# Strassen's seven products in the first MLP matmul of a fused vision block

## The chip, the cores and the metric

The kernel runs on one core of a Trainium2 chip. The core has a matmul engine (TensorE, PE in the profile), two elementwise engines that can read the matmul's result memory PSUM (VectorE, DVE; ScalarE, ACT), one that works on SBUF only in this kernel (GpSimd, POOL), and a queue that issues most DMAs (SyncE, SP). Each engine works through its own instructions in program order, and waits on semaphores for what others produce. The metric is the device time of one execution in microseconds (us); lower is better.

## The reference

Two transformer-like layers work on an image batch of 2 x 56 x 56 tokens with 384 channels, all in float32. The first is neighbourhood attention and an MLP. The second is a convolution with four running averages, a projection, and an MLP. Its end, which is where the change lies, is this:

```python
mixed = 0.25 * (lr + rl + tb + bt) + local            # 768 channels per token
mixed = _layernorm(mixed, on_g, on_b)
x = x + (mixed @ w_out + b_out)                       # 768 -> 384
h2 = _layernorm(x, n2_g, n2_b)
m = jax.nn.gelu(h2 @ w1 + b1, approximate=False) @ w2 + b2   # 384 -> 1536 -> 384
return x + m
```

## The kernel before

The 6272 tokens of the second layer's end are cut into groups (`dgroups`): twelve of 512 tokens, which are four token tiles of 128, and a last one of 128. The loop over groups is at lines 1614 to 1645 for groups 0 to 5 and at lines 1659 to 1684 for groups 6 to 12 (`half_way` is 6). For each group g there are four pieces of work:

- **The hidden layer.** `hT` holds the normalized input of the group with channels on the partitions, three blocks of 128 channels. `columns` (L1092) makes one tile of 128 hidden channels by 512 tokens in a PSUM bank: three matmuls, one per channel block, with a 128x128 piece of `w1` as weights and 512 columns of `hT`. `hidden` then has ScalarE apply the gelu (L1103). There are twelve such tiles. From group 6 on they are made in an order (L1664) that completes two tiles of the lower half of the hidden channels and two of the upper half together, because `sums_of_hidden` (L1526) has GpSimd make sums of these for the second matmul.
- **Measuring.** Beside the hidden layer of group g, the mean and variance of `mixed` are taken for the tokens of group g + 1. From group 7's tokens on this is `measure_by_vector` (L1315): VectorE turns each token tile in sixteen 32-row transposes (L1320) and takes two statistics (L214) and one aggregate (L215). `Norm.close` turns variances into factors: one VectorE instruction (L219), then a power on GpSimd (L222).
- **`project_out`** (L1341) multiplies `mixed` of group g + 1 by `w_out`, token tile by token tile (L1110), adds the residual on VectorE with the measured factor (L1347), and measures the result for the next norm.
- **`tokens_by_seven`** (L1533) is the second matmul of the MLP of group g. It already uses Strassen's seven block products, with the blocks being halves of the tokens, of the hidden channels and of the output channels. Between these products it prepares the next group's `hT`: ScalarE normalizes (L240), VectorE transposes (`turned`, L1076), ScalarE scales by the norm's gain and bias (`scaled`, L1083). It ends with adds into the result and one output DMA.

The program order within each engine is written out by hand: the order of the Python calls is the order of the instructions. A PSUM bank that is named again waits for its last reader. Before group 6 the PSUM pools are rearranged (L1647 to 1658): one bank, `bank_b`, is written to zero by a matmul with zeros, so that later matmuls may add to what ScalarE copies into it. The GpSimd sums of `w2` for the seven products are made at the start of group 5 (`sums_of_w2`, L1516), behind the add of a row to the next input tile (`add_row`, L1028).

Of the kernel before, what the change touches and what calls it, by code (L numbers as in the profile page):

```python
# [33 lines left out]
F32 = mybir.dt.float32  # L34
AF = mybir.ActivationFunctionType
# [7 lines left out]
P = 128  # L43
# [130 lines left out]
def block_kernel(ctx: ExitStack, tc: tile.TileContext, ins: dict, out: bass.AP):  # L174
# [26 lines left out]
    class Norm:  # L201
# [12 lines left out]
                nc.vector.bn_stats(st[:n, i, :], x)  # L214
            nc.vector.bn_aggr(self.mv[:n, k, :], st[:n, : len(parts), :])  # L215

        def close(self, k, n=P):
            rs = self.rs[:n, :k]
            nc.vector.scalar_tensor_tensor(  # L219
                rs, self.mv[:n, :k, 1], EPS, ones[:n, :k], ALU.add, ALU.mult  # L220
            )
            nc.gpsimd.tensor_tensor(rs, rs, mhalf[:n, :k], ALU.pow)  # L222

        def apply(self, k, x, out):
            n = x.shape[0]
# [755 lines left out]
    def passes(xs, xn, w1, w2, between=lambda ps: None):  # L981
# [32 lines left out]
        def bank():  # L1014

            turns.append(0)
            in_turn = bank_b is None and len(turns) % 2 == 1
            return y_end if in_turn else ps_y.tile([P, C], F32, name="y")

        turns, hids, bank_b = [], [], None  # L1020

        def row(name):
            return rows[:, 1 if name == "b_out" else 0, :]
# [61 lines left out]
                    scale=col(g, c),  # L1085
                )

        def columns(w, m, hT, n):

            ps = ps_m.tile([P, MT], F32, name="mm")  # L1090
            for c in range(NC):
                nc.tensor.matmul(  # L1092
                    ps[:, : n * P], lhsT=w[:, c, m * P : (m + 1) * P], rhs=hT[:, c, : n * P],
                    start=c == 0, stop=c == NC - 1,
                )
            return ps

        def hidden(w1, m, hT, n, b1):
            ps = columns(w1, m, hT, n)
# [214 lines left out]

        def measure_by_vector(mx, norm, k):  # L1315

            t = tp.tile([P, NI * P], F32, name="turned", bufs=2)
            for i in range(0, P, HD):
                for j in range(0, P, HD):
                    nc.vector.transpose(  # L1320
                        t[j : j + HD].rearrange("p (m c) -> p m c", m=NI)[:, :, i : i + HD],
                        mx[i : i + HD, :, k * P + j : k * P + j + HD],
                    )
            norm.add(k, [t[:, h * C : (h + 1) * C] for h in range(2)])

        def measure_beside(m, g, ahead):


            n = dgroups[g][1]
            if g > half_way:  # L1330
                if m % 2 == 0 and m // 2 < n:
                    measure_by_vector(ahead[0], ahead[2], m // 2)
            else:
                late = 2 if g == half_way else 0
                k = (m - late) // 2 - 1
                if m % 2 == 1 and 0 <= k < n:
                    measure(ahead[0], ahead[2], k)
            if m == (NHID - 1 if g == half_way else 10):
                ahead[2].close(n)

        def project_out(g, mx, x, inner):  # L1341
            n = dgroups[g][1]
            x3 = io.tile([P, NT, C], F32, name="xc")
            norm = Norm(sm)
            for k in range(n):
                ps = tokens([mx[:, c, :] for c in range(NI)], w_out, k)
                nc.vector.scalar_tensor_tensor(  # L1347
                    x3[:, k, :], ps, inner.rs[:, k : k + 1], x[:, k, :], ALU.mult, ALU.add
                )
                norm.add(k, [x3[:, k, :]])  # L1350
                beside.go(OUT_D)
            norm.close(n)
            return x3, norm
# [159 lines left out]
        project_in(g, hT, first_input)  # L1513
        n2 = "L1_conv_n2_g", "L1_conv_n2_b"

        def sums_of_w2(w2):  # L1516

            q = NHID // 2
            b11, b12 = w2[:, :q, : C // 2], w2[:, :q, C // 2 :]
            b21, b22 = w2[:, q:, : C // 2], w2[:, q:, C // 2 :]  # L1520
            t1, t2, t3, t4 = (tp.tile([P, q, C // 2], F32, name=f"w2_t{i}") for i in range(4))
            for to, x, y in ((t1, b12, b11), (t2, b22, t1), (t3, b22, b12), (t4, b21, t2)):
                nc.gpsimd.tensor_tensor(to, x, y, ALU.subtract)
            return t1, t2, t3, t4
# [8 lines left out]
        def tokens_by_seven(t0, low, high, s1, s2, w2, w2_sums, res, g, x_next, norm):  # L1533
# [8 lines left out]
            bank_a = ps_d.tile([P, 2, hc], F32, name="ya")  # L1542
# [3 lines left out]
            more = g + 1 < dlast  # L1546
# [53 lines left out]
            for p in range(2):  # L1600
                product(bank_b, p, of(high, 1), t4)
            scaled(hT, n_next, *n2)
            add_row(x_next, n_next, "b2_1")
            nc.vector.tensor_tensor(quarter(1, 0), bank_b, quarter(1, 0), ALU.add)
            for p in range(2):
# [6 lines left out]
            return hT  # L1612
        hT = channels(first["xn"], dgroups[0][1], *n2)
        for g, (t0, n) in enumerate(dgroups[:half_way]):
            if g == half_way - 1:

                cctx.close()
                tp = pctx.enter_context(tc.tile_pool(name="tail", bufs=1, reuse_waits="tile"))
                w2_sums = sums_of_w2(w2)
            hid = []  # L1620
            for m in range(NHID):
                hid.append(hidden(w1, m, hT, n, "L1_conv_b1"))
                measure_beside(m, g + 1, ahead)
                beside.go(MLP_D)
            res = x3
            x3, norm = project_out(g + 1, *ahead)
            if g + 2 != half_way:
                ahead = load_mix(g + 2)
            for k in range(n):
                if k == n - 1:  # L1630
                    hT = channels(xn, dgroups[g + 1][1], *n2)
                ps = tokens(hid, w2, k)
                o = res[:, k, :]
                if k == 0:
                    norm.shift(dgroups[g + 1][1])
                nc.vector.tensor_tensor(o, ps, o, ALU.add)
# [8 lines left out]


        bctx.close()  # L1647
        ps_y = pctx.enter_context(tc.tile_pool(name="psy2", bufs=2, space=PSUM))
        ps_m = pctx.enter_context(tc.tile_pool(name="psm2", bufs=3, space=PSUM))
        ps_d = pctx.enter_context(tc.tile_pool(name="psd", bufs=1, space=PSUM))  # L1650
        HALVES, HC = 2, C // 2
        bank_b = ps_d.tile([P, HALVES, HC], F32, name="yb")
        zeros = tp.tile([P, C], mybir.dt.bfloat16, name="zeros")
        nc.vector.memset(zeros, 0.0)

        nc.tensor.matmul(
            bank_b.rearrange("p t c -> p (t c)"), lhsT=zeros[:, :P], rhs=zeros, start=True, stop=True
        )
        for g, (t0, n) in enumerate(dgroups):
            if g < half_way:  # L1660
                continue
            hid = {}
            first_pair = len(hids)
            for i, m in enumerate(m for u in range(3) for m in (2 * u, 2 * u + 1, 6 + 2 * u, 7 + 2 * u)):  # L1664
                hid[m] = hidden(w1, m, hT, n, "L1_conv_b1")
                if g < dlast:
                    measure_beside(i, g + 1, ahead)
                    if i % 4 == 3:
                        if i == 3:
                            s1, s2 = (tp.tile([P, NHID // 2, MT // 2], F32, name=x) for x in ("s1", "s2"))  # L1670
                        sums_of_hidden(i // 4, *hids[-2:], s1, s2)
            res = x3
            if g < dlast:
                x3, norm = project_out(g + 1, *ahead)
            if g + 2 <= dlast:
                ahead = load_mix(g + 2)
            if g == dlast:
                for k in range(n):
                    ps = tokens([hid[m] for m in range(NHID)], w2, k, y_end)
                nc.vector.tensor_copy(rows[:, 1, :], res[:, n - 1, :])  # L1680
                assert n == 1 and t0 + n * P == T2
                break
            pairs = hids[first_pair:]
            hT = tokens_by_seven(t0, pairs[::2], pairs[1::2], s1, s2, w2, w2_sums, res, g, x3, norm)
        pctx.close()

    def raise_flag(ps):
# [89 lines left out]
```

## Time and profile before

| | us |
|---|---|
| Median of 3 runs (2639.23 to 2642.07) | 2639.56 |
| The profiled execution, whole | 2640.17 |
| Its span in the profile | 2638.4 |

Busy time in single groups of the second half of the loop, from the stage view of the profile (from one group's first matmul to the next group's):

| group | stretch, us | PE | DVE | ACT | POOL | PE clock |
|---|---|---|---|---|---|---|
| 6 | 2188.41 to 2262.09 | 73.68 | 55.69 | 13.26 | 25.34 | 1.00 |
| 8 | 2335.78 to 2409.45 | 73.67 | 56.54 | 14.38 | 26.33 | 1.00 |
| 10 | 2483.13 to 2556.81 | 73.68 | 54.18 | 15.45 | 23.86 | 1.00 |
| 11 | 2556.81 to 2618.88 | 62.07 | 15.43 | 11.45 | 19.48 | 1.00 |

Columns are microseconds in which the engine was busy. Group 11 is shorter because the group after it has only one token tile to project. Busy time of PE is that of pipelined records: how fast matmuls follow each other is read from start to start. Rows of the profile name the source line, the engine, the operation, the tile written and the tiles read, the shapes, and how many instructions are merged; in square brackets stands the idle time of the engine before the row and what ended it.

### The profile page before, as it was taken

Reading aid. Unit: us, or ns where it says so; the run is one execution under the profiler, and the core shown is the slowest. Engines: PE = TensorE matmul, PEld = TensorE weight load, DVE = VectorE, ACT = ScalarE, POOL = GpSimd, SP = SyncE. Lnnn points to the kernel's source line nnn. Section 1 sums busy time; section 2 is a strip of 40 time slices with the busy share of each in tenths; the row PEclk is TensorE's granted clock in tenths of the full one; section 3 lists DMA queues with packets and bytes.
Section 4 is the critical chain, followed back from the end, with each engine's and each line's share of the span. In section 5 each row is a group of like instructions: output and inputs, shape, how many; then the busy total and the mean of one; then the engine's idle time right before and its main releaser. Section 6 shows DMA issues by size and latency. Waiting matters only on the chain. (4 is left out here: it accounts for less than half of the span.)

```text
span 2638.4 us, 38178 instructions
## 1 busy us (share of the span) xinstructions
PE 2613.8 (99%) x15420; PEld 1520.5 (58%) x15420; DVE 1961.9 (74%) x3540; ACT 906.9 (34%) x1465; POOL 365.6 (14%) x370
## 2 busy tenths in 40 slices
PE   9999999999999999999999999999999999999999
PEld 5666556666655445555555555555555555666777
DVE  3778777876465688688988889889988825788761
ACT  4555555554323333223334423212233311122111
POOL 0111111110211100000010000000010032333332
PEclk9999999999999999999999999999999999999999
DMA  6423354224511122233345535533264321111000
GB/s 217 138 91 98 125 185 162 81 81 144 180 37 39 64 90 102 95 116 111 121 142 214 209 125 184 181 119 120 102 220 164 143 94 42 48 48 48 22 12 17
DMA packets 131644, 299.05 MB, mean 113 GB/s; under 512 B 10390, under 2 KB 86528, under 8 KB 129152
## 3 DMA queue, kind: packets, MB, share of 16 engines
q1 hardware_dynamic: 126512, 269.76, 29.8%
q10 hardware_dynamic: 4944, 26.74, 2.9%
q8 instruction: 123, 2.02, 0.3%
q14 instruction: 65, 0.53, 0.1%
HBM read 180.86 MB, written 115.61 MB: 112 GB/s over the span
## 5 line engine op out<-in xcount | busy, mean ns | idle before, releaser
L1092 PE MATMUL mm<-hT,w 128*128 128x512 f32 (+3 forms) x1872 | 769.5, 568 | 0.4 <-ACT hT L254 0.2
L1092 PEld LDWEIGHTS mm<-hT,w 128*128 128x128 f32 x1872 | 346.4, 190 | 386.8 <-issue 364.7
L1103 ACT ACTIVATE hid<-mm,chan 128x512 f32<-128x512 f32 (+3 forms) x312 | 206.1, 661 | 659.5 <-PE mm L1092 659.5
L1188 DVE SCALAR_TENSOR_TENSOR loc<-pt,taps,loc 128x990 f32<-128x990 f32 (+9 forms) x336 | 377.1, 1122 | 10.0 <-ACT loc L1170 1.7
L1110 PE MATMUL y_end<-w,hid 128*128 128x384 f32 x912 | 300.3, 486 | 0.0
L1110 PE MATMUL y<-w,hid 128*128 128x384 f32 x864 | 284.5, 486 | 0.0
L222 POOL TENSOR_TENSOR rs<-rs,mhalf 128x4 f32<-128x4 f32 (+4 forms) x67 | 87.3, 1303 | 1418.7 <-DVE rs L219 1383.3
L531 DVE TENSOR_TENSOR pts<-sc,bias 119x448 f32<-119x448 f32 (+3 forms) x336 | 220.8, 699 | 72.1 <-PE sc L516 70.0
L537 ACT ACTIVATE pts<-pts 119x448 f32<-119x448 f32 (+3 forms) x336 | 206.6, 642 | 183.4 <-DVE pts L531 183.3
L1110 PEld LDWEIGHTS y_end<-w,hid 128*128 128x128 f32 x912 | 172.7, 190 | 118.8
L1110 PEld LDWEIGHTS y<-w,hid 128*128 128x128 f32 x864 | 163.5, 190 | 112.5 <-issue 1.0
L387 PE MATMUL ps<-hT,wqkv 128*128 128x448 f32 x504 | 211.9, 559 | 7.1 <-ACT vs L432 5.0
L1076 DVE STREAM_TRANSPOSE hT<-xn 32x96 f32<-32x96 f32 x672 | 181.2, 270 | 38.1 <-ACT xn L240 17.7
L1092 PE MATMUL mm<-hT,w_in 128*128 128x512 f32 (+2 forms) x468 | 191.9, 568 | 0.6 <-ACT hT L254 0.6
L1092 PEld LDWEIGHTS mm<-hT,w_in 128*128 128x128 f32 x468 | 88.5, 190 | 102.1 <-issue 90.4
L387 PEld LDWEIGHTS ps<-hT,wqkv 128*128 128x128 f32 x504 | 90.0, 190 | 87.8 <-issue 72.2
L1110 PE MATMUL y<-w_out,mx 128*128 128x384 f32 x420 | 138.7, 486 | 0.0
L516 PEld LDWEIGHTS sc<-qT,kT 32*100 32x100 f32 (+3 forms) x3168 | 90.7, 169 | 66.9 <-issue 15.5
L1320 DVE STREAM_TRANSPOSE turned<-mx 32x192 f32<-32x192 f32 x336 | 123.3, 367 | 4.2
L240 ACT ACTIVATE xn<-xc,sh,rs 128x384 f32<-128x384 f32 x98 | 64.7, 698 | 168.4 <-DVE sh L233 168.3
L516 PE MATMUL sc<-qT,kT 32*100 32x112 f32 (+3 forms) x3168 | 113.4, 270 | 6.5 <-DVE pts L531 5.2
L1110 PEld LDWEIGHTS y<-w_out,mx 128*128 128x128 f32 x420 | 79.7, 190 | 57.7 <-issue 5.3
(134 smaller groups left out, 3104.3 us busy)
## 6 DMA issues: line engine op xcount, KB each, us to landing
loc<-loc_d SPq DMA_DIRECT2D x24, 784.0 KB
mixed<-mix_d SPq DMA_DIRECT2D x24, 784.0 KB
mix_d<-mixed SPq DMA_DIRECT2D x24, 784.0 KB
xa<-x_d SPq DMA_DIRECT2D x23, 768.0 KB
bias<-in_bias_t ACTq DMA_DIRECT2D x13, 1344.0 KB
mx<-mix_d SPq DMA_DIRECT2D x11, 1536.0 KB
p_d<-mx SPq DMA_DIRECT2D x10, 1536.0 KB
pt<-p_d SPq DMA_DIRECT2D x18, 560.0 KB
```

The lines of the kernel that those rows point to most:

```text
L222: nc.gpsimd.tensor_tensor(rs, rs, mhalf[:n, :k], ALU.pow)
L240: nc.scalar.activation(out[:, k, :], x[:, k, :], AF.Identity, bias=self.sh[:n, k : k + 1], scale=self.rs[:n, k : k + 1],)
L387: nc.tensor.matmul(ps, lhsT=wqkv[:, c, m * P : (m + 1) * P], rhs=hT[:, c, half_of(n)], start=c == 0, stop=c == NC - 1,)
L516: nc.tensor.matmul(sc[i // 2][: w.keys, i % 2, (first + c) * TT : (first + c + 1) * TT], lhsT=kT[d, hg, w.keys_at + r * w.kc : w.keys_at + ...
L531: nc.vector.tensor_tensor(self.of(half), sc[half][:n, :, at].rearrange("p h (c q) -> p h c q", q=TT), self.w.bias[:n, 4 * self.hg + h : 4 ...
L537: nc.scalar.activation(self.of(half), self.of(half), AF.Exp)
L1076: nc.vector.transpose(hT[j : j + HD, :, k * P + i : k * P + i + HD], xn[i : i + HD, k, :].rearrange("p (c q) -> p c q", c=NC)[:, :, j : j ...
L1092: nc.tensor.matmul(ps[:, : n * P], lhsT=w[:, c, m * P : (m + 1) * P], rhs=hT[:, c, : n * P], start=c == 0, stop=c == NC - 1,)
L1103: nc.scalar.activation(t[:, : n * P], ps[:, : n * P], AF.Gelu, bias=col(b1, m))
L1110: nc.tensor.matmul(ps, lhsT=t[:, k * P : (k + 1) * P], rhs=w[:, m, :], start=m == 0, stop=m == len(lhs) - 1,)
L1188: nc.vector.scalar_tensor_tensor(to, pt[:, lo + dy - self.top : hi + dy - self.top, xt : xt + n], self.tap(dy, dx), to, ALU.mult, ALU.add,)
L1320: nc.vector.transpose(t[j : j + HD].rearrange("p (m c) -> p m c", m=NI)[:, :, i : i + HD], mx[i : i + HD, :, k * P + j : k * P + j + HD],)
```

## The change

The first MLP matmul of groups 6 to 11 is computed in another way. The 512 tokens are split into halves a and b, the 1536 hidden channels into a lower and an upper half, and the first two of the three channel blocks of `hT` serve as the two halves of the summed dimension. For these, seven block products replace eight. The third channel block is added to the four results by plain matmuls. All matmuls of this step have 256 columns. The hidden channels are made in three units u of two lower and two upper tiles. In each, a PSUM bank collects the product that all four results share; ScalarE copies it into another bank (which, like `bank_b`, has been set to zero by a matmul beforehand), and copies intermediate sums from there to SBUF; VectorE adds from PSUM to these. The gelu runs on half tiles. The last part of a unit (`finish`) is issued inside the next unit, and the third unit's in `project_out` of the next group after its first token tile.

Five sums of `w1` blocks (768 columns each) are made by GpSimd once, in group 5 before those of `w2`; four sums of `hT` (256 columns each) once per group, at the end of `tokens_by_seven`. Measuring by VectorE is issued in half tiles: three token tiles beside the hidden layer and the fourth inside `project_out`, with its own `close`. The PSUM banks change: `bank_a` of `tokens_by_seven` is now the bank that `project_out` also uses, `project_out` alternates between that bank and `y_end`, and the last group's hidden tiles have two banks where they had three.

```diff
-        def close(self, k, n=P):
-            rs = self.rs[:n, :k]
+        def close(self, k, n=P, first=0):
+            rs = self.rs[:n, first:k]
...
-        def project_out(g, mx, x, inner):
+        def project_out(g, mx, x, inner, then=lambda k: None):
...
                 norm.add(k, [x3[:, k, :]])
+                then(k)
...
+        def sums_of_w1(w1):
+            h = HID // 2
+            b11, b12 = w1[:, 0, :h], w1[:, 0, h:]
+            b21, b22 = w1[:, 1, :h], w1[:, 1, h:]
...
+            for to, x, y in (
+                (t1, b12, b11), (t2, b22, t1), (t3, b22, b12), (t4, b21, t2),
+                (other, w1[:, 2, :h], w1[:, 2, h:]),
+            ):
+                nc.gpsimd.tensor_tensor(to, x, y, ALU.subtract)
...
+        def sums_of_input(hT):
+            a, b = slice(0, MT // 2), slice(MT // 2, MT)
+            t = tp.tile([P, 4, MT // 2], F32, name="xsums", bufs=1)
+            for to, x, y, op in (
+                (t[:, 0], hT[:, 0, b], hT[:, 1, b], ALU.add),
+                (t[:, 1], t[:, 0], hT[:, 0, a], ALU.subtract),
+                (t[:, 2], hT[:, 0, a], hT[:, 0, b], ALU.subtract),
+                (t[:, 3], hT[:, 1, a], t[:, 1], ALU.subtract),
+            ):
+                nc.gpsimd.tensor_tensor(to, x, y, op)
+            return t
...
+            def add(bank, u, w, x, start=False):
+                for i in range(2):
+                    m = 2 * u + i
+                    nc.tensor.matmul(
+                        bank[:, i, :], lhsT=w[:, m * P : (m + 1) * P], rhs=x,
+                        start=start and i == 0, stop=True, skip_group_check=True,
+                    )
...
+            def finish(u):
+                bank = banks_b[u % 2]
+                gelu(high[u], b, u2[u], 6 + 2 * u)
+                add(bank, u, t4, hT[:, 1, b])
+                add(bank, u, other, hT[:, 2, b])
+                gelu(low[u], b, bank, 2 * u)
+                add(z[u], u, w1[:, 1, h:], xsums[:, 3])
+                add(z[u], u, w1[:, 2, h:], hT[:, 2, a])
+                nc.vector.tensor_tensor(u1[u], z[u], u1[u], ALU.add)
+                gelu(high[u], a, u1[u], 6 + 2 * u)
+                sums_of_hidden(u, low[u], high[u], *s12)
+
+            for u in range(3):
...
+                add(bank_a, u, w1[:, 0, :h], hT[:, 0, a], True)
+                nc.scalar.copy(bank, bank_a)
+                add(z[u], u, t1, xsums[:, 0], True)
+                next(measuring, None)
+                if u:
+                    finish(u - 1)
+                add(bank, u, t2, xsums[:, 1])
+                nc.scalar.copy(u1[u], bank)
+                add(bank_a, u, w1[:, 1, :h], hT[:, 1, a])
+                add(bank_a, u, w1[:, 2, :h], hT[:, 2, a])
+                gelu(low[u], a, bank_a, 2 * u)
+                next(measuring, None)
+                add(bank, u, t3, xsums[:, 2])
+                add(bank, u, w1[:, 2, h:], hT[:, 2, b])
+                nc.scalar.copy(u2[u], bank)
+                nc.vector.tensor_tensor(u2[u], z[u], u2[u], ALU.add)
...
             scaled(hT, n_next, *n2)
+            xsums = sums_of_input(hT) if n_next == NT else None
             add_row(x_next, n_next, "b2_1")
...
-                w2_sums = sums_of_w2(w2)
+                w1_sums, w2_sums = sums_of_w1(w1), sums_of_w2(w2)
...
+            low, high, finish = hidden_by_seven(
+                hT, xsums, w1, w1_sums, (s1, s2), measure_by_steps(ahead, range(min(n_next, 3)))
+            )
+            ahead[2].close(min(n_next, 3))
+            more = measure_by_steps(ahead, range(3, n_next))
+
+            def then(k):
+                if k == 0:
+                    finish()
+                next(more, None)
+                if k == 1 and n_next > 3:
+                    ahead[2].close(n_next, first=3)
```

More of the change, by code (lines that the diff above doesn't have):

```diff
@@ L215, in add @@
             nc.vector.bn_aggr(self.mv[:n, k, :], st[:n, : len(parts), :])
-        def close(self, k, n=P):
-            rs = self.rs[:n, :k]
+        def close(self, k, n=P, first=0):
+            rs = self.rs[:n, first:k]
             nc.vector.scalar_tensor_tensor(
-                rs, self.mv[:n, :k, 1], EPS, ones[:n, :k], ALU.add, ALU.mult
+                rs, self.mv[:n, first:k, 1], EPS, ones[:n, first:k], ALU.add, ALU.mult
             )
-            nc.gpsimd.tensor_tensor(rs, rs, mhalf[:n, :k], ALU.pow)
+            nc.gpsimd.tensor_tensor(rs, rs, mhalf[:n, first:k], ALU.pow)
         def apply(self, k, x, out):
@@ L1016, in bank @@
             turns.append(0)
-            in_turn = bank_b is None and len(turns) % 2 == 1
-            return y_end if in_turn else ps_y.tile([P, C], F32, name="y")
-        turns, hids, bank_b = [], [], None
+            return y_end if len(turns) % 2 == 1 else ps_y.tile([P, C], F32, name="y")
+        turns, hids = [], []
         def row(name):
@@ L1086, in scaled, with columns @@
                 )
-        def columns(w, m, hT, n):
-            ps = ps_m.tile([P, MT], F32, name="mm")
+        def columns(w, m, hT, n, name="mm"):
+            ps = ps_m.tile([P, MT], F32, name=name)
             for c in range(NC):
@@ L1096, in columns, with hidden @@
             return ps
-        def hidden(w1, m, hT, n, b1):
-            ps = columns(w1, m, hT, n)
+        def hidden(w1, m, hT, n, b1, name="mm"):
+            ps = columns(w1, m, hT, n, name)
             if m % 2 == 0:
@@ L1323, in measure_by_vector @@
                     )
+                if i == HD:
+                    yield
             norm.add(k, [t[:, h * C : (h + 1) * C] for h in range(2)])
+            yield
         def measure_beside(m, g, ahead):
             n = dgroups[g][1]
[L1330 to L1337, printed above, removed]
+            late = 2 if g == half_way else 0
+            k = (m - late) // 2 - 1
+            if m % 2 == 1 and 0 <= k < n:
+                measure(ahead[0], ahead[2], k)
             if m == (NHID - 1 if g == half_way else 10):
                 ahead[2].close(n)
-        def project_out(g, mx, x, inner):
+        def project_out(g, mx, x, inner, then=lambda k: None):
             n = dgroups[g][1]
@@ L1514, in passes, with measure_by_steps @@
         n2 = "L1_conv_n2_g", "L1_conv_n2_b"
+        def measure_by_steps(ahead, tiles):
+            for k in tiles:
+                yield from measure_by_vector(ahead[0], ahead[2], k)
+        def sums_of_w1(w1):
+            h = HID // 2
+            b11, b12 = w1[:, 0, :h], w1[:, 0, h:]
+            b21, b22 = w1[:, 1, :h], w1[:, 1, h:]
+            three = wp.tile([P, NC, INNER], F32, name="w1_t", tag="w_in")
+            t1, t2, t3 = (three[:, c, :] for c in range(NC))
+            t4, other = (tp.tile([P, h], F32, name=x) for x in ("w1_t4", "w1_other"))
+            for to, x, y in (
[3 more added lines that the diff above has]
+                nc.gpsimd.tensor_tensor(to, x, y, ALU.subtract)
+            return t1, t2, t3, t4, other
@@ new lines, in hidden_by_seven, with gelu @@
+        def hidden_by_seven(hT, xsums, w1, w1_sums, s12, measuring):
+            h, mh = HID // 2, MT // 2
+            a, b = slice(0, mh), slice(mh, MT)
+            t1, t2, t3, t4, other = w1_sums
+            low, high, z, u1, u2 = [], [], [], [], []
+            def add(bank, u, w, x, start=False):
[5 more added lines that the diff above has]
+                    )
+            def gelu(to, part, src, m):
+                for i in range(2):
+                    nc.scalar.activation(
+                        to[:, i, part], src[:, i, :], AF.Gelu, bias=col("L1_conv_b1", m + i)
+                    )
[11 more added lines that the diff above has]
+            for u in range(3):
+                bank = banks_b[u % 2]
+                bank_a = ps_u.tile([P, 2, mh], F32, name="ua", bufs=1)
+                z.append(ps_u.tile([P, 2, mh], F32, name="uz"))
+                u1.append(tp.tile([P, 2, mh], F32, name="hid_u1", bufs=2))
+                u2.append(tp.tile([P, 2, mh], F32, name="hid_u2", bufs=2))
+                low.append(gp.tile([P, 2, MT], F32, name="hid", tag="hid"))
+                high.append(gp.tile([P, 2, MT], F32, name="hid", tag="hid"))
+                add(bank_a, u, w1[:, 0, :h], hT[:, 0, a], True)
[14 more added lines that the diff above has]
+                nc.vector.tensor_tensor(u2[u], z[u], u2[u], ALU.add)
+            return low, high, lambda: finish(2)
@@ L1541, in tokens_by_seven @@
             t1, t2, t3, t4 = w2_sums
-            bank_a = ps_d.tile([P, 2, hc], F32, name="ya")
+            bank_a = ps_y.tile([P, C], F32, name="y").rearrange("p (t c) -> p t c", t=2)
             bank_z = y_end.rearrange("p (t c) -> p t c", t=2)
@@ L1545, in tokens_by_seven @@
             n_next = dgroups[g + 1][1]
-            more = g + 1 < dlast
             def of(tiles, half):
@@ L1611, in tokens_by_seven @@
             )
-            return hT
+            return hT, xsums
         hT = channels(first["xn"], dgroups[0][1], *n2)
@@ L1647, in passes @@
         bctx.close()
-        ps_y = pctx.enter_context(tc.tile_pool(name="psy2", bufs=2, space=PSUM))
-        ps_m = pctx.enter_context(tc.tile_pool(name="psm2", bufs=3, space=PSUM))
+        ps_y = pctx.enter_context(tc.tile_pool(name="psy2", bufs=1, space=PSUM))
         ps_d = pctx.enter_context(tc.tile_pool(name="psd", bufs=1, space=PSUM))
-        HALVES, HC = 2, C // 2
+        ps_u = pctx.enter_context(tc.tile_pool(name="psu", bufs=2, space=PSUM))
+        ps_m = ps_u
+        HALVES, HC, MH = 2, C // 2, MT // 2
         bank_b = ps_d.tile([P, HALVES, HC], F32, name="yb")
-        zeros = tp.tile([P, C], mybir.dt.bfloat16, name="zeros")
+        banks_b = [ps_d.tile([P, HALVES, MH], F32, name=f"ub{i}") for i in range(2)]
+        zeros = tp.tile([P, MT], mybir.dt.bfloat16, name="zeros")
         nc.vector.memset(zeros, 0.0)
-        nc.tensor.matmul(
-            bank_b.rearrange("p t c -> p (t c)"), lhsT=zeros[:, :P], rhs=zeros, start=True, stop=True
-        )
+        for t in (bank_b, *banks_b):
+            flat_t = flat(t)
+            nc.tensor.matmul(
+                flat_t, lhsT=zeros[:, :P], rhs=zeros[:, : flat_t.shape[1]], start=True, stop=True
+            )
+        xsums = sums_of_input(hT)
         for g, (t0, n) in enumerate(dgroups):
@@ L1661, in passes @@
                 continue
[L1662 to L1671, printed above, removed]
+            if g == dlast:
+                hid = [hidden(w1, m, hT, n, "L1_conv_b1", "uz") for m in range(NHID)]
+                for k in range(n):
+                    ps = tokens(hid, w2, k, y_end)
+                nc.vector.tensor_copy(rows[:, 1, :], x3[:, n - 1, :])
+                assert n == 1 and t0 + n * P == T2
+                break
+            n_next = dgroups[g + 1][1]
+            s1, s2 = (tp.tile([P, NHID // 2, MH], F32, name=x) for x in ("s1", "s2"))
+            low, high, finish = hidden_by_seven(
+                hT, xsums, w1, w1_sums, (s1, s2), measure_by_steps(ahead, range(min(n_next, 3)))
+            )
+            ahead[2].close(min(n_next, 3))
[6 more added lines that the diff above has]
+                    ahead[2].close(n_next, first=3)
             res = x3
-            if g < dlast:
-                x3, norm = project_out(g + 1, *ahead)
+            x3, norm = project_out(g + 1, *ahead, then)
             if g + 2 <= dlast:
                 ahead = load_mix(g + 2)
[L1677 to L1684, printed above, removed]
+            hT, xsums = tokens_by_seven(t0, low, high, s1, s2, w2, w2_sums, res, g, x3, norm)
         pctx.close()
```

## The prediction

> **What bounds the kernel now.** I read the engines' busy shares first, then TensorE's order of work in one late group, then the rows of the other engines around the moments at which TensorE needs something.
>
> ```profile
> span 2638.4 us, 38178 instructions
> PE 2613.8 (99%) x15420; PEld 1520.5 (58%) x15420; DVE 1961.9 (74%) x3540; ACT 906.9 (34%) x1465; POOL 365.6 (14%) x370
> ```
>
> TensorE (PE) is busy 99% of the span, at a granted clock of 1.00 in every stage, so a matmul less is time less, if nothing makes PE wait instead. The stage that changes is groups 6 to 11. Group 8 on PE (start us, us, what):
>
> ```profile
> 2335.78 31.06 PE L1092 MATMUL mm<-hT,w 128*128 128x512 f32 x72
> 2366.68 15.64 PE L1110 MATMUL y<-w_out,mx 128*128 128x384 f32 x48
> 2382.16 4.06 PE L1556 MATMUL ya<-w,hid 128*128 128x192 f32 x24
> ...
> 2405.55 4.06 PE L1556 MATMUL y_end<-w,hid 128*128 128x192 f32 x24
> ```
>
> From start to start: 30.90 us for the hidden layer, 15.48 for `project_out`, 27.29 for `tokens_by_seven`; the next group starts at 2409.45, 73.67 later, with no gap. Each matmul of the program is two records here. The cover is thin, though. The same group's last VectorE and ScalarE rows:
>
> ```profile
> 2382.36 0.62 DVE L1347 SCALAR_TENSOR_TENSOR xc<-y,rs,xa 128x384 f32<-128x384 f32 x1 [2.44 <-PE y L1110]
> 2385.12 3.39 DVE L233 SCALAR_TENSOR_TENSOR sh<-mv,rs 128x4 f32<-128x4 f32 x1 [1.13 <-POOL rs L222]
> 2389.28 13.58 DVE L1076 STREAM_TRANSPOSE hT<-xn 32x96 f32<-32x96 f32 x48 [0.78 <-ACT xn L240]
> 2403.83 4.50 DVE L1076 STREAM_TRANSPOSE hT<-xn 32x96 f32<-32x96 f32 x16
> 2408.37 2.23 ACT L1083 ACTIVATE hT<-hT,chan 128x512 f32<-128x512 f32 x3 [7.99 <-DVE hT L1076]
> ```
>
> The chain from the last add of `project_out` (0.2 us after PE's last token tile) through the norm, 64 transposes and the scaling reaches channel block 0 at about 2409.17; PE begins to load for 2409.45 at 2409.29. The reserve is some 0.1 us: whatever delays the 2382.36 row costs nearly its full length, in each group.
>
> **Matmuls removed.** Before: 12 tiles x 3 blocks = 36 matmuls of 512 columns, 72 records at 30.90/72 = 0.429 us. After: 11 calls of `add` per unit x 2 x 3 units = 66 matmuls of 256 columns, 132 records. The kernel has that shape once, in its first layer's 256-token group:
>
> ```profile
> 700.30 15.86 PE L1092 MATMUL mm<-hT,w 128*128 128x256 f32 x72 [0.22 <-ACT hT L254]
> 716.09 0.19 PE L1688 MATMUL y_end<-ones,bad 128*1 128x1 f32 x2
> ```
>
> 15.79/72 = 0.219, with two waits of 0.16 us in its weight loads; a straight line through the 512 and 192 column rows (0.429, 0.1625) gives 0.216. I take 0.217: 132 x 0.217 = 28.6, so 2.3 us less a group, 13.6 over six. Ends: 0.216 (14.4 in all) and 0.222 (9.6), the pace of the 36 `w_in` records of 256 columns, 7.99 us from start to start.
>
> Here a rule speaks against the change. The Trainium skill, "TensorE: Matmul & The Clock Gate", section "Back-to-back issue gap", puts a stream of weight load and matmul pairs at about 81 ns a matmul for 128 columns and 131 for 512, so that halving the columns is far from halving the time. Interpolated (my estimate) a 256-column record would cost 98/131 = 0.75 of a 512 one: 132 x 0.75 x 0.429 = 42.5 us, 11.6 more per group, 70 in all. The rows say 0.219/0.429 = 0.51, and 192 columns run at 0.1625 with a weight load of 190 ns in each record, overlapped. I follow the rows.
>
> **Sums of w1, on GpSimd, once, in group 5.** The five sums go in front of the four w2 sums; behind these stands the power that ends the measuring norm (start us, us):
>
> ```profile
> 2134.92 2.62 POOL L1523 TENSOR_TENSOR w_t<-w,w_t 128x1152 f32<-128x1152 f32 x1
> 2140.88 1.02 POOL L222 TENSOR_TENSOR rs<-rs,mhalf 128x4 f32<-128x4 f32 x1 [3.33 <-DVE rs L219]
> ```
>
> A 768-wide `tensor_tensor` of GpSimd took 1.81 (the 128x768 `xa` row), five make 9.1. The w2 sums then end at 2146.7 instead of 2137.5, the power at 2147.8, the first add of `project_out` (0.62, L1347) at 2148.4. PE wants that add's bank for token tile 2 at 2147.21 and gets it at about 2148.6 with the weight load (0.2): 1.4 lost. The second rule weighed: "SBUF — State Buffer", section "Who interferes with whom", lets a VectorE instruction with two SBUF inputs and a GpSimd one that reads SBUF exclude each other. The `rs` instruction before the power (L219, 0.16 at 2140.64) is such a one and now falls into that run. By its own row it is done in time: 1.4; by the rule it may wait until the run ends: 1.7. I take 1.5. No other DMA or queue moves past it.
>
> **Zeroing** three banks for one: two more matmuls of 512 bf16 columns, a memset twice as long (0.22 now): 0.5 once. Group 6's own input sums run on GpSimd 7 us before PE is there: nothing.
>
> **Input sums, groups 7 to 11.** Four GpSimd operations of 256 columns (0.73 each, L1564) after the scaling. The first needs blocks 0 and 1, scaled at about 2409.88 (2408.37 + 0.80 + 0.71): done at 2410.7, its matmul at 2410.9. PE arrives after one `add` (2 x 2 x 0.217 = 0.87) at 2410.3: 0.6 us wait. The next three come each 0.73 later, in time. 5 x 0.6 = 3.0; ends 0.3 and 0.9. They push `add_row` (3.44) and the last add some 8 us back, and the output store with them on SyncE's queue, ahead of loads that are wanted a group later: nothing.
>
> **Within a unit (9.5 us of PE).** ScalarE is first in, first out: `copy` to u1 stands behind the two gelus that wait for VectorE's add into u1. From the end of the second z product: 0.2 to VectorE, 0.68 the add (0.61 at 448 wide, 0.85 at 672, L531), 0.07, two gelus 0.86 (0.474 each, L1103 at 256), copy 0.5 net (0.48 at 384 wide, plus 128 columns, less overlap), 0.2 to PE: 2.55. PE has three `add` in between: 2.60. Nothing to spare; I take 0.05 for each of 12 (units 1 and 2 of six groups): 0.6, ends 0 and 0.3 each.
>
> VectorE per unit: one tile's measuring 7.27 (16 transposes 6.06, two stats, one aggregate) and two adds 1.36: 8.6 of 9.5. It fits: the piece of 8 transposes ends 0.8 before the add that PE needs.
>
> **`project_out`** now holds the third unit's end (4 `add`, 3.5 us) and the fourth tile's measuring. From its start on PE: add of tile 0 at 4.1; z product ends 7.3; add into u1 to 8.2; half tile to 11.3; tile 1's add 11.4, stats to 12.75; half tile, stats, close to 17.3; tile 2's add and stats to 18.7; tile 3's add is due at 19.1. VectorE has caught up by 0.4, so the chain to the next group starts as before: 0. The bank that `tokens_by_seven` takes over is that of tile 2, read by 18.0, needed at 18.9: 0. The last group's two banks instead of three: 0.67 us of PE a tile against 0.2 + 0.37 + 0.1: 0.
>
> **Sum:** -13.6 + 1.5 + 0.5 + 3.0 + 0.6 = -8.0. The profiled execution took 2640.17 (span 2638.4 and 1.8 around it); it becomes 2632.2. The median of the runs shown is 2639.56, 0.6 below that execution: 2631.6.
>
> **Rivals.** (1) As summed, 0.60: 2631.6, own range 2628.5 to 2634.5. (2) The waits are shorter than the rows make them (input sums 0.3, unit waits 0, group 5 costs 1.0, records 0.216): -14.4 + 1.0 + 0.5 + 1.5 = -11.4, 2628; 0.13. For it: all bounds on latency are mine. (3) Tile 3's add comes late by 1.5 against a reserve of 0.4: 1.1 x 5 = 5.5 back, 2637; 0.20. For it: reserve 0.1 in the chain; against: VectorE idles 17 of 73.7 us. (4) Slower, 0.07: VectorE paces the units. Its place is the step of 8.6 against 9.5; every 1 us over 9.5 costs 18 us (three units, six groups), so it decides from 9.9 a step, where the 8.0 are gone. If the adds took 1.7 each, because beside GpSimd they wait like the 3.39 row, the step is 10.7: 1.2 x 18 = 21.6, so +13, 2653. Against: the adds have one input in PSUM, and L1598 took 0.55 beside a GpSimd operation. That the change does not happen is no case: 66 matmuls of 256 columns per group stand in PE's order.
>
> **Numbers.** About 0.2% (5.3 us) is what a measurement can tell: below 2634.3 is faster. Case 1 gives 0.58 of its 0.60, case 2 0.13, case 3 0.03: 0.74; within: 0.18; slower 0.08. The range 2627.5 to 2637.5 takes in the ends of cases 1 to 3 and leaves out case 4 and the worst of 3.
>
> **What would show it.** After: 256-column records at 0.217; about 0.6 us of PE idle put down to GpSimd's input sums at five group starts; 1.5 at the third token tile of group 5's `project_out`; group period near 72. Wrong if PE waits for ScalarE's copies by more than 0.3 in each unit, or if the next group's transposes start later after tile 3's add in `project_out` than the 6.9 us seen here (2382.36 to 2389.28).

## Result and profile after

| | before | after |
|---|---|---|
| Median of 7 runs each, us | 2641.06 (2639.22 to 2642.38) | 2631.53 (2628.70 to 2634.81) |
| Profiled execution, us | 2640.17 | 2631.16 |
| Its span, us | 2638.4 | 2629.4 |

The ratio is 0.9967, with a 95% interval of 0.9955 to 0.9978: 9.5 us faster. The forecast was 2631.6, with 2627.5 to 2637.5 as its range. The total is right, in part because the median of before is 1.5 us higher here than over the three runs that the forecast started from (2641.06, not 2639.56); several of its terms are not, as the following shows.

The page of the kernel after, its span and busy times by engine:

```profile
span 2629.4 us, 39158 instructions
...
PE 2603.2 (99%) x15781; PEld 1590.3 (60%) x15782; DVE 1987.7 (76%) x3581; ACT 949.1 (36%) x1591; POOL 392.7 (15%) x404
```

There are about 360 more matmul records on PE, 6 x (132 - 72), and yet 10.6 us less of PE's busy time: shape decides what a record costs. ScalarE, GpSimd and VectorE got 42, 27 and 26 us more. The stage view of group 8, first in the columns of the table of before (stretch, us, then busy time and instructions of PE, PEld, DVE, ACT, POOL, then the clock, the DMA share and GB/s):

```profile
2334.16:2406.00 71.84, 71.54 (x350) 61.43 (x349) 60.37 (x166) 21.44 (x44) 29.53 (x26) 1.00 0.13 45
```

The period is 71.84 instead of 73.67, and for the first time in these groups PE's busy time is below it: 0.30 is a gap. PE's order of work at the start of group 9 shows where (start us, us, what, idle time before it and what ended it):

```profile
2406.00 1.03 PE L1564 MATMUL ua<-hT,w 128*128 128x256 f32 x4
2407.35 1.13 PE L1564 MATMUL uz<-xsums,w_t 128*128 128x256 f32 x4 [0.32 <-POOL xsums L1545]
2408.31 1.03 PE L1564 MATMUL ub<-xsums,w_t 128*128 128x256 f32 x4
2409.18 1.89 PE L1564 MATMUL ua<-hT,w 128*128 128x256 f32 x8
2410.90 1.03 PE L1564 MATMUL ub<-xsums,w_t 128*128 128x256 f32 x4
```

Undisturbed, four records follow in 0.86 (2409.18 to 2410.90 is eight in 1.72). From 2406.00 to 2407.35 it is 1.35, so the wait is 0.48 (by the unrounded starts), of which the page calls 0.32 idle; and the four records behind the wait take 0.96, another 0.10. Hence the input sums cost 0.58 here. A wait costs more than its idle time.

### The account, term by term

Two stretches are compared. The whole span moved by -9.0 us, but the unchanged part ahead of the change took 1.04 longer in this execution: group 5's first transpose into `xi`, just before anything differs, starts at 2121.39 before and at 2122.43 after. From there to the end of the last instruction (2638.37 and 2629.36), called **the tail** from here on, it is 516.98 before and 506.93 after: **-10.05**.

| term | forecast | measured in the trace after |
|---|---|---|
| matmuls | -13.6 | -14.4: 132 records at 0.2159 are 28.5, against 30.90; six times |
| sums of w1 in group 5 | +1.5 | +0.9 |
| zeroing | +0.5 | +0.5 |
| input sums | +3.0, five starts of 0.6 | +2.3, four starts of 0.58 |
| waits within units | +0.6 | 0.3: two waits for the copy behind the second sum's product, in groups 6 and 11 |
| two banks in the last group | 0 | +0.4 |
| tile 3's add in `project_out` | 0 | 0 |
| **sum** | **-8.0** | **-10.0** |

The last column adds to what the tail shows. The last group's term is read from its twelve hidden tiles: they take 8.42 from start to start of the two rows below, where three banks took 8.04.

PE's order of work in the last group, after:

```profile
2609.50 8.58 PE L1091 MATMUL uz<-hT,w 128*128 128x128 f32 x72
2617.92 7.91 PE L1109 MATMUL y_end<-w,hid 128*128 128x384 f32 x24
```

### The profile page after: what moved, and what is told of

Its sections match the earlier page's. It is cut to its first block, busy times and chain, and to the rows that moved or that the text cites. A ratio compares the mean times of both kernels' runs of the same rounds, so it can differ in the third digit from the quotient of the medians.

```text
span 2629.4 us, 39158 instructions
## 1 busy us (share of the span) xinstructions
PE 2603.2 (99%) x15781; PEld 1590.3 (60%) x15782; DVE 1987.7 (76%) x3581; ACT 949.1 (36%) x1591; POOL 392.7 (15%) x404
## 5 line engine op out<-in xcount | busy, mean ns | idle before, releaser
L1091 PE MATMUL mm<-hT,w 128*128 128x512 f32 (+2 forms) x1368 | 575.0, 576 | 0.4 <-ACT hT L254 0.2
L1091 PEld LDWEIGHTS mm<-hT,w 128*128 128x128 f32 x1368 | 256.6, 190 | 286.0 <-issue 265.9
L1102 ACT ACTIVATE hid<-mm,chan 128x512 f32<-128x512 f32 (+2 forms) x228 | 152.2, 668 | 503.4 <-PE mm L1091 503.4
L557 PE MATMUL o<-pts,vt 100*32 100x112 f32 (+3 forms) x3168 | 111.1, 264 | 1.2 <-ACT og L479 1.0
L425 PE MATMUL ps<-wqkv,hT 128*128 128x384 f32 x294 | 106.9, 502 | 0.0
```

What stands on the lines that cost most here:

```text
L425: nc.tensor.matmul(ps, lhsT=hT[:, c, at : at + P], rhs=wqkv[:, c, 2 * C :], start=c == 0, stop=c == NC - 1,)
L557: nc.tensor.matmul(o[i * HD : (i + 1) * HD, hg, :], lhsT=w.vt[:n, c, h * HD : (h + 1) * HD], rhs=self.pts[:n, i, c, :], start=c == 0, stop ...
L1091: nc.tensor.matmul(ps[:, : n * P], lhsT=w[:, c, m * P : (m + 1) * P], rhs=hT[:, c, : n * P], start=c == 0, stop=c == NC - 1,)
```

## Experiments

The theory is the account: matmuls at 0.2159 gain 14.4, and five small losses, each a wait or work at one place, give 4.4 back. It has three rivals: that taking a loss away brings nothing, as something else is late next; that it hardly matters where the measuring is placed, as VectorE has idle time; and that the 256-column shape itself costs much, as the back-to-back rule has it. The whole times of single executions turned out to move by several us for a reason outside the change (last section), so an edit is judged by the tail of its profiled execution, with the ratio to before of the whole times beside it. That is one execution per kernel; how far it can be trusted stands below the table.

| kernel | median us (range, runs) | ratio to before (95%) | tail us |
|---|---|---|---|
| row_later | 2631.47 (2629.13 to 2632.89, 4) | 0.9957 (0.9940 to 0.9973) | 505.37 |
| w1_sums_later | 2632.17 (2627.87 to 2634.70, 5) | 0.9953 (0.9938 to 0.9969) | 506.06 |
| measure_later | 2646.94 (2641.22 to 2652.67, 12) | 1.0020 (1.0011 to 1.0030) | 521.67 |
| measure_and_row_later | 2636.05 (2630.03 to 2640.64, 7) | 0.9968 (0.9954 to 0.9983) | 508.15 |
| before_in_halves | 2643.07 (2637.58 to 2648.77, 20) | 1.0002 (0.9994 to 1.0010) | 518.06 |
| before_row_later | 2640.32 (2637.99 to 2647.55, 12) | 0.9997 (0.9988 to 1.0006) | 516.99 |
| all_mended | 2628.84 (2624.34 to 2634.49, 6) | 0.9947 (0.9932 to 0.9962) | 503.84 |

The kernel before had 2641.74 (2637.58 to 2646.68, 19 runs) beside the first four and 2642.41 (2637.06 to 2650.05, 35 runs) beside the others.

Most of the tail repeats to a few hundredths of a us: groups 7 to 10 take 73.67 to 73.68 each in before and before_row_later, 71.84 to 71.86 after and 71.85 to 71.86 in w1_sums_later. One term does not. Group 5's wait for the sums of `w1` costs 0.90 after, but 1.15 in row_later, 1.33 in measure_later and 1.51 in measure_and_row_later, which have the same instructions there. GpSimd's run of sums stands behind an `add_row` that waits for the load of its input tile, and that add begins 2.12 us behind the marker after, and 2.38, 2.56 and 2.72 behind it in the other three. So up to 0.6 us between these four tails is no effect of an edit; it is taken out below where it matters.

### row_later: is the wait for the input sums on the path?

The trace after shows what makes the chain to `hT` so late that PE must wait for the sums. VectorE's shift, which takes 0.16 by itself, runs beside GpSimd's add of a row to the next input tile. GpSimd and VectorE, at the end of `project_out` in group 9:

```profile
2453.51 3.44 POOL L1027 TENSOR_TENSOR xa<-xa,rows 128x1536 f32<-128x1536 f32 x1
2453.58 3.39 DVE L233 SCALAR_TENSOR_TENSOR sh<-mv,rs 128x4 f32<-128x4 f32 x1 [1.12 <-POOL rs L222]
```

The two begin and end together. The edit moves that add to a point from which nothing needs GpSimd soon:

```diff
-            if g >= half_way:
+            if g >= half_way and not late:
                 add_row(x, dgroups[g][1], "b_out")
...
             last_sum(0)
+            meanwhile()
...
-                ahead = load_mix(g + 2)
+                ahead = load_mix(g + 2, late=True)
+                meanwhile = lambda: add_row(ahead[1], dgroups[g + 2][1], "b_out")
```

> The changed kernel, with the row add to the input tile after next (GpSimd, 3.44 us) moved behind the first last_sum of tokens_by_seven, so that the norm's shift on VectorE (3.39 us beside it, 0.16 alone) is not held up. Theory (the wait at four group starts is the lateness of the chain shift, normalize, transposes, scaling, then 0.73 us of input sum): the chain comes 3.2 us earlier, the wait of 0.3 us on GpSimd's input sums goes from all four starts, each group period falls from 71.85 to about 71.4, and the time by 1.8 us to some 2629.7. Rival (the input sums are slow for themselves, as GpSimd is late whatever the chain does): the wait and the time stay, 2631.5.

The tail became 1.56 shorter, though group 5 took 0.25 longer: without that it is 1.81, as expected, and the group period is 71.40. The same places in its trace, VectorE, GpSimd and PE:

```profile
2380.61 0.16 DVE L233 SCALAR_TENSOR_TENSOR sh<-mv,rs 128x4 f32<-128x4 f32 x1 [1.12 <-POOL rs L222]
...
2403.91 0.73 POOL L1545 TENSOR_TENSOR xsums<-hT 128x256 f32<-128x256 f32 x1 [4.81 <-ACT hT L1082]
...
2404.89 1.03 PE L1564 MATMUL ua<-hT,w 128*128 128x256 f32 x4
2405.76 1.03 PE L1564 MATMUL uz<-xsums,w_t 128*128 128x256 f32 x4
2406.67 1.10 PE L1564 MATMUL ub<-xsums,w_t 128*128 128x256 f32 x4
2407.61 1.89 PE L1564 MATMUL ua<-hT,w 128*128 128x256 f32 x8
```

The shift is 0.16, the first input sum begins 1.0 ahead of PE instead of 0.6 behind (2406.57 after), and PE has no idle before `uz`. The chain came 1.5 earlier, not the 3.2 that were expected: ScalarE copies a product of `tokens_by_seven` first (L1672), which PE completes only now, so normalizing starts at 2382.07 although the shift ends at 2380.78. So the loss of the input sums was on the path, and what set it was the shift held up beside GpSimd's add, not the pace of the four sums. The rival, that they are slow for themselves, falls. What is late next is little: the next two groups of four records take 0.91 and 0.94 instead of 0.86, 0.13 per start. That the shift falls to 0.16 once GpSimd is idle is what the Trainium skill, "SBUF — State Buffer", section "Who interferes with whom", has for a VectorE instruction with two SBUF inputs.

### before_row_later: the same edit without the change

> The kernel before, with the row add moved behind the first last_sum. Theory (there the chain just reached its group start, TensorE had no gap): VectorE's shift falls from 3.39 to 0.16 us, the next input is ready 3 us earlier, and the time stays, 2641 within 1 us. Rival (the shift's delay was already paid before): 2 us or more faster.

The tail is 516.99 against 516.98. The shift is 0.16 here too (at 2384.03), and the scaling starts 2.6 instead of 1.1 us ahead of PE's next group; yet before the change PE wasn't waiting for it: the edit pays only because the change made the chain end at GpSimd's sums.

### w1_sums_later: the five sums of group 5

In the trace after the measuring norm's power stands behind nine sums on GpSimd, and PE waits for the add behind it. GpSimd, VectorE and PE in group 5:

```profile
2144.75 2.61 POOL L1620 TENSOR_TENSOR w_t<-w,w_t 128x1152 f32<-128x1152 f32 x1
2147.32 1.02 POOL L222 TENSOR_TENSOR rs<-rs,mhalf 128x4 f32<-128x4 f32 x1
2148.38 0.62 DVE L1346 SCALAR_TENSOR_TENSOR xc<-y,rs,xa 128x384 f32<-128x384 f32 x1 [6.14 <-POOL rs L222]
...
2149.05 4.14 PE L1109 MATMUL y<-w_out,mx 128*128 128x384 f32 x12 [0.63 <-DVE xc L1346]
```

The edit makes the w1 sums after `project_out`, and leaves the w2 sums where they were:

```diff
-                w1_sums, w2_sums = sums_of_w1(w1), sums_of_w2(w2)
+                w2_sums = sums_of_w2(w2)
...
             x3, norm = project_out(g + 1, *ahead)
+            if g == half_way - 1:
+                w1_sums = sums_of_w1(w1)
```

> The changed kernel, with the five sums of w1 issued on GpSimd behind project_out of group 5 instead of in front of the w2 sums. Theory (the measuring norm's power waits in GpSimd's queue behind the nine sums): the idle time of TensorE before the third token tile of that project_out (0.63 us put down to VectorE, 0.9 with the restart) goes, and the time falls by 0.9 to about 2630.6; the input sums of group 6 stay hidden. Rival (the sums are needed there, or their move holds up the next shift and the row adds): TensorE waits elsewhere before group 6 by 1 us or more, no gain or a loss.

The tail is 0.87 shorter. PE's four token tiles start 3.87 apart in that trace, without a gap: the account's 0.9 was on the path, and PE waits for nothing new before group 6.

### measure_later: how much the half-tile cut and its place are worth

The change issues the fourth tile's measuring from the first token tile of `project_out` on. This edit starts it one tile later, and changes nothing else:

```diff
                 if k == 0:
                     finish()
-                next(more, None)
-                if k == 1 and n_next > 3:
+                else:
+                    next(more, None)
+                if k == 2 and n_next > 3:
                     ahead[2].close(n_next, first=3)
```

> The changed kernel, with the two halves of the fourth tile's measuring issued after token tiles 1 and 2 of project_out instead of after 0 and 1; the same instructions in all. Theory (VectorE's chain from the last add of project_out to the next input has no reserve, so a late last add costs its full length): the last add comes about 3.3 us late, groups 6 to 9 lose that much and group 10 about 2.4 (its row add is short, so it has a reserve), 15.6 in all: about 2647, slower than the kernel before. Rival (the chain is hidden, as VectorE idles some 11 us a group): within 2 us of 2631.5.

The tail is 14.74 longer (14.3 without group 5's share), and the kernel as a whole is slower than before (1.0020, 1.0011 to 1.0030): the placing of one tile's measuring is worth more than the change itself. The last add of `project_out` now waits for its factor instead of for PE. VectorE, after and then in this kernel, one group apart:

```profile
2450.83 0.62 DVE L1346 SCALAR_TENSOR_TENSOR xc<-y_end,rs,xa 128x384 f32<-128x384 f32 x1 [0.47 <-PE y_end L1109]
```

```profile
2386.60 0.62 DVE L1346 SCALAR_TENSOR_TENSOR xc<-y_end,rs,xa 128x384 f32<-128x384 f32 x1 [0.67 <-POOL rs L222]
```

In the first row the factor lies ready and VectorE idles 0.47 for PE: that is the reserve which the prediction put at 0.4. In the second the power is late, and the delay comes out at PE's next group, of which this kernel's order of work shows:

```profile
2407.84 4.14 PE L1651 MATMUL y_end<-w,hid 128*128 128x192 f32 x24 [0.80 <-DVE u L1689]
2413.48 1.13 PE L1564 MATMUL ua<-hT,w 128*128 128x256 f32 x4 [1.50 <-ACT hT L1082]
2414.99 1.13 PE L1564 MATMUL uz<-xsums,w_t 128*128 128x256 f32 x4 [0.38 <-POOL xsums L1545]
```

The group's period is 75.11 (from `uz` at 2339.88 to 2414.99), 3.3 more than after, as expected. Group 10 and the start of group 11 together lose 1.4, less than the 2.4 that were expected. That VectorE is idle for a good part of a group doesn't make the place of its work free: the second rival falls.

### measure_and_row_later: are the two costs one chain?

Both edits together.

> Both edits: the row add behind the first last_sum and the fourth tile's measuring one token tile later. Theory (the one gives back 3.2 us of reserve, the other takes 3.3): the group starts are where they are in the changed kernel, with about 1.6 more in group 10; 2632 to 2634, that is 13 to 15 us faster than with the measuring moved alone. Rival (what the late measuring costs has another way than this chain, such as the banks of project_out): most of the 15.6 us stays, 2645 or more.

The tail is 508.15, 1.22 longer than after, of which 0.61 is group 5, though the measuring alone cost 14.74 and the row alone gained 1.56. They don't add: the shift and the late measuring lie on one chain. The last add still waits 0.67 for the power in this trace (at 2387.99), but the shift behind it is 0.16 (at 2390.74) instead of about 3.4, and PE's next group starts without idle time of PE. What the late measuring still costs has another way, and there the rival is right in small: PE's second product in `tokens_by_seven` writes `y_end`, the bank that the late last add has just read, and so starts 0.29 late (2388.66) and gets under way 0.1 more slowly, 0.4 in each of five groups. The 1.6 that were expected in group 10 did not come: from its start to that of group 11 it takes 71.87, against 71.85 after.

### before_in_halves: the shape without the seven products

The kernel before, each 512-column matmul of groups 6 to 11's hidden layer made as two of 256 columns:

```diff
+            if bank_b is not None and n == NT:
+                for c in range(NC):
+                    for i in range(2):
+                        nc.tensor.matmul(
+                            ps[:, i * 2 * P : (i + 1) * 2 * P], lhsT=w[:, c, m * P : (m + 1) * P],
+                            rhs=hT[:, c, i * 2 * P : (i + 1) * 2 * P],
+                            start=c == 0 and i == 0, stop=c == NC - 1, skip_group_check=True,
+                        )
+                return ps
```

> The kernel before, with each hidden matmul of 512 columns in groups 6 to 11 made as two of 256: the same products, 144 records in place of 72 a group, no sums. Theory (a matmul's time is its columns and a fixed 2.5 ns a record, weight loads overlap): 144 x 0.2159 = 31.1 against 30.9 us, 0.2 a group, 1 us in all: about 2642. Rival (weight loads set the pace, 0.75 of a 512 column record for half of it): 46 us a group, over 90 us more in all.

PE's order of work in group 8:

```profile
2341.72 31.24 PE L1094 MATMUL mm<-hT,w 128*128 128x256 f32 x144
2372.80 7.58 PE L1119 MATMUL y<-w_out,mx 128*128 128x384 f32 x23
```

144 records in 31.08 is 0.2158 each, against 30.90 for 72 of 512 columns. The tail grew by 1.08, six times this 0.18; over 72 more records a group that is 2.5 ns for each. Had the rule of the Trainium skill, "TensorE: Matmul & The Clock Gate", section "Back-to-back issue gap", held for this stream, 72 x 2 x 0.75 x 0.429 = 46.3 would stand in place of 31.08. The third rival falls; the weight loads (PEld 61 of 71.8 us in a group after) stay hidden.

### all_mended: the losses taken out together

row_later, w1_sums_later, and a third bank for the last group's hidden tiles, which is `ua` at that time:

```diff
-                hid = [hidden(w1, m, hT, n, "L1_conv_b1", "uz") for m in range(NHID)]
+                hid = [hidden(w1, m, hT, n, "L1_conv_b1", ("uz", "uz", "ua")[m % 3]) for m in range(NHID)]
```

> The changed kernel with the row add later, the w1 sums later, and a third bank for the last group's hidden tiles. Theory (the three waits are separate places on TensorE's path): 1.8 + 0.9 + 0.4 = 3.1 us less than the changed kernel, about 2628.4; the last group's hidden tiles take 8.04 us again from start to start, against 8.42. Rival (the gains are not additive, since a wait that goes uncovers another one): under 1.5 us less than the changed kernel.

The tail is 503.84: 3.09 less than after and 13.14 less than before. The ratio to before is 0.9947 (0.9932 to 0.9962); its interval overlaps that of the changed kernel, so the whole times alone would not tell the two apart. The stage view of group 7, and PE in the last group:

```profile
2267.73:2339.13 71.40, 71.40 (x350) 61.42 (x349) 57.25 (x166) 21.51 (x43) 29.49 (x27) 1.00 0.13 45
```

```profile
2613.11 1.50 PE L1091 MATMUL uz<-hT,w 128*128 128x128 f32 x12
...
2621.14 7.91 PE L1109 MATMUL y_end<-w,hid 128*128 128x384 f32 x24
```

PE is busy for the whole of the group again, and the last group's tiles are back at 8.03. The three parts sum to 1.81 (the row without group 5's share) + 0.87 + 0.4 = 3.08, and 3.09 was measured: they add up, so they are separate waits, and what came late behind them is no more than the 0.13 per start seen in row_later: the first rival falls. By the tail this version is the fastest of all.

## Why the prediction was right, and where its terms were off

**What bounds.** Right: PE's work less is time less. Of 14.4 us of matmuls 10.0 came through, and the 4.4 that did not are the five losses of the table, three of which the runs took out.

**Matmuls, -13.6.** The mechanism was right, the record mis-sized: 0.2159 rather than 0.217, over 6 x 132 records 0.8 to 0.9. The straight line through the 512 and 192 column rows had given 0.216; I moved off it towards a row that held two waits (the `w_in` row behind the 0.222 held some at its start, too, and runs at 0.216 behind them). Following the rows against the back-to-back rule was right, and before_in_halves shows it without the rest of the change.

**Input sums, 5 x 0.6.** The size was right (0.58), the count wrong: four. At group 11's start PE does not wait for them. Its chain is earlier, since the row added to the one-tile group is 384 wide; GpSimd and VectorE after:

```profile
2525.37 1.00 POOL L1027 TENSOR_TENSOR xa<-xa,rows 128x384 f32<-128x384 f32 x1
2525.43 0.95 DVE L233 SCALAR_TENSOR_TENSOR sh<-mv,rs 128x4 f32<-128x4 f32 x1 [1.12 <-POOL rs L222]
```

The trace of before had a shift of 0.95 in that place already; I took group 8's chain for all five. And the step named GpSimd's 0.73 per sum as the price without asking what made `hT` late: row_later shows that it was the 3.39 of a row which the prediction itself printed.

**Sums of w1, 1.5.** Right mechanism, 0.9 in this execution (removing them gained 0.87); the same code lost 1.15 to 1.51 in three others, so the 1.5 is the upper end of what was seen, and one trace of before could not tell how far the term moves. Here the power came about 0.5 earlier than forecast: 0.16 of it because GpSimd's run happened to start earlier than before, most of the rest because nine sums and the power follow each other more closely than their durations add up (768 columns: 1.77 from start to start, not 1.81; the power begins as the last sum ends). And the weight load of 0.2 had been done during the wait. The 0.10 by which PE runs slower behind a wait was missing in the other direction. The rule on exclusion, weighed for the L219 row, did bite: 0.55 instead of 0.16, but early enough to be off the path. The forecast let it last until the run of sums ends; it lasted only until the sum under way had ended (last section).

**Zeroing, 0.5, and `project_out`, 0.** Right. The reserve of tile 3's add was 0.47 (forecast 0.4), the transposes start 6.92 after it (2450.83 to 2457.75), as before, and measure_later shows how thin that is: with one token tile less of lead, the third rival (tile 3 late) would have been the case, at more than twice its price.

**Within a unit, 0.05 for each of 12.** Too much. ScalarE's copy in the later units arrives in time, if with little to spare, as "nothing to spare" had it: in group 9 it ends at 2420.11, and its matmul starts at 2420.40 when the `add` ahead of it is through (2418.67 and twice 0.86). Where PE does wait for such a copy, in group 11, its matmul starts 0.14 behind the copy's end (2551.35 to 2551.49), so here about 0.15 was left. What was missed is that the first unit of a group can wait for its copy when the group starts without another wait: 0.2 in group 6 and 0.1 in group 11.

**The last group's two banks, 0.** Wrong: 0.4. The estimate of 0.67 for a round of the bank (0.2 + 0.37 + 0.1) against 0.67 of PE a tile left nothing to spare, and I counted that as hidden. Measured are 8.42/12 = 0.70 a tile; all_mended's third bank brings back 0.67.

**The sum.** The tail gained 10.0 where 8.0 was forecast, and the profiled execution came out only 1.0 below the 2632.2 because its unchanged part happened to be 1.04 longer. The medians fell by 9.5, from a start that was 1.5 higher than the forecast's. So the mechanism was right, and the nearness of the totals (2631.53 and 2631.6) is luck. The likeliest case, with its own range of 2628.5 to 2634.5, held; VectorE did not pace the units: it is busy for 60.4 us of 71.8, and PE waits for none of its adds within the units.

## What to carry to other kernels

When matmuls are cut on a bound PE, price the new ones from rows of their own shape, from start to start, and then find what each new operand waits for: here all the losses were waits at a group's edges (a start, a last group, a set-up), none in the middle. If a short VectorE instruction takes as long as the GpSimd instruction beside it, move the latter before trying to speed up the chain in another way; check first that something waits for that chain, or it brings nothing. Check the short groups at the end separately from the typical one. And before a difference of some tenths of a us between two traces is put down to an edit, look for waits that move in code that the edit left alone: here one moved by 0.6 with the landing of a load.

## What was not expected of the hardware

- **The unchanged part moves more than most edits.** The first MLP matmul of the first layer, with the same work before it in all kernels, starts between 698.79 and 707.67 us in the nine profiled executions, 8.9 us apart, as much as the change brings. In this part the traces show stretches of 3.4 us in which TensorE's granted clock is 0.50 (from 26.00 to 29.40 us in the trace after, for one): none in the two executions that start earliest (698.79 and 699.23), one in the next two (before and row_later), two after (701.38), and 13.65 us of them in each of the four latest (703.50 to 707.67). At half speed these 13.65 cost at most 6.8, so they explain most of the spread, not all. Each stretch follows TensorE waits that make up 1.2 to 2.9 us of the 3.4 ahead of it; but the same waits stand in executions whose clock stays at 1.00, and what decides is open. From a marker behind that part, edits were told apart that are 1 us in size, once group 5's own spread was known. PE after, and then at the same place in before_row_later:

```profile
318.98 4.22 PE L387 MATMUL ps<-hT,wqkv 128*128 128x448 f32 x6 [1.85 <-ACT vs L432]
```

```profile
317.80 2.52 PE L387 MATMUL ps<-hT,wqkv 128*128 128x448 f32 x6 [1.81 <-ACT vs L432]
```

- **A wait costs PE about 0.1 more than its length.** The four records behind a wait of 0.48 took 0.96 where 0.86 is their pace, and the twelve behind group 5's wait 3.97 instead of 3.87. The first record carries it, and it is nearly the same for every shape: over the nine traces the record behind the one that waited starts 0.32 after it where 0.216 is the pace (256 columns), 0.43 for 0.32 (384) and 0.53 for 0.43 (512). Why is not shown.
- **VectorE got in between two GpSimd instructions.** L219 waited while GpSimd ran its sums, and finished at 2142.24 as one of them ended (2142.21) and the next began; it did not wait for the whole run. In row_later, measure_later and measure_and_row_later, where the sums begin later against it, it took 0.80, 0.98 and 1.15, and each time ended 0.03 or less behind the end of the sum under way. The rows, VectorE and GpSimd after:

```profile
2141.69 0.55 DVE L219 SCALAR_TENSOR_TENSOR rs<-mv,ones 128x4 f32<-128x4 f32 x1
```

```profile
2139.59 2.62 POOL L1620 TENSOR_TENSOR w_t<-w,w_t 128x1152 f32<-128x1152 f32 x1
2142.18 2.60 POOL L1620 TENSOR_TENSOR w_t<-w 128x1152 f32<-128x1152 f32 x1
```
